# Position terms of an attention kernel: the row axis copied straight from PSUM, the column axis alone through DRAM

## The chip, the cores and the metric

The kernel runs on one NeuronCore of a Trainium2 chip. The metric is the device time of one execution in microseconds (us). Before the change it is 4188.24 us, the median of 3 runs that range from 4181.4 to 4191.72 us. The engines are TensorE (PE: matmuls; PEld: its weight loads), VectorE (DVE), ScalarE (ACT), GpSimd (POOL) and SyncE (SP), which here only issues DMAs. An engine takes its instructions in the order in which the program gave them to it. All data are float32.

## The reference

Two layers, each for 4 images of 32 x 32 tokens with 768 channels. A layer normalizes its input by groups of channels, projects it to queries, keys and values of 12 heads of 64, and attends over all 1024 tokens of an image. To the scores it adds two position terms, one for the distance in rows and one for that in columns, each a product of the query with a table of 63 relative distances (27 in layer 1, with the ends repeated):

```python
x = x + _L0_conv_ref(_gn(x), ...)          # layer 0; layer 1 is alike, with biases
# inside a layer, B*12 heads, S = H*W = 1024 tokens
rel_h = einsum('bhwc,hkc->bhwk', r_q, Rh)  # Rh[i, j] = rel_pos_h[i - j + H - 1]
rel_w = einsum('bhwc,wkc->bhwk', r_q, Rw)
bias = (rel_h[..., :, None] + rel_w[..., None, :]).reshape(B * hn, S, S)
attn = softmax(scale * einsum('bqc,bkc->bqk', q, k) + bias)
out = einsum('bqk,bkc->bqc', attn, v) ... @ Wproj + bproj
```

## The kernel before, in words

There are 8 images to work through (4 images, 2 layers), each with 6 pairs of heads; a pair is g = 0 to 47. A pair has 8 blocks of 128 queries, n = 0 to 7, and the main loop (line 705) goes through the 384 steps (g, n). The whole order is written out by hand: every engine's queue is filled in the order of this loop.

**One step (g, n).** `biases` (line 452) builds the sum of both position terms for the step after next on GpSimd, two operations of 128 x 1024. `scores` (line 466) does the matmuls of the next step; VectorE evicts them with the bias and the row's minimum (line 482), ScalarE takes the exponential and its sum (line 486). `turn` (line 501) transposes the step's attention weights in 32 x 32 blocks on VectorE into a buffer tb (line 513); after two steps, a quarter of the pair, SyncE writes tb to a DRAM scratch td (line 516) and one or two steps later reads it back as pt (`read_back`, line 524), in the layout that the weighting wants. tb has 3 buffers, and a quarter takes two. `divide` (line 491) multiplies the next step's weights by the inverse sum, one head on GpSimd, one on ScalarE. `weigh` multiplies pt with the values on TensorE (line 543): quarters 0 and 1 of a pair in step 6, quarters 2 and 3 in step 2 of the next pair.

**Fillers.** Beside this, the steps of pair g do the projections of pair g + 1 and, in four groups per pair, the output projection of this or the last image. They are generators in a list; `take(todo, n)` draws n pieces of them, by the table `shares` with one number per step. `project_in` (line 245) projects q and k in four units; for most pairs by a scheme with sums of weights (made by `sum_weights`, line 314, on ScalarE and GpSimd in steps 6 and 7 of the pair before) and sums of inputs (`sum_input`, line 333), which is a Winograd form of the 2 x 2 block product: 7 half products in place of 8. `plain(g)` pairs, the first of each image and pair 1, don't use it. `project_values` (line 361) does the values, `project_out` (line 611) the output. In an image's fifth pair VectorE normalizes the next image's input (line 226), 12 applies of 128 x 512; in its sixth pair `sum_input` makes the input's sums.

**Position terms.** `positions(g, i)` (line 398) multiplies half of the queries with the table: 64 distances of the row axis and 64 of the column axis for each query and head, in one PSUM tile of 128 x 2 x 4 x 128 (tp, line 409; tp0 and tp1 are the two tiles of a pair). ScalarE copies it to SBUF in two parts (line 419) and writes both to a DRAM scratch tdr (line 421). `diagonals(g)` (line 428) then reads from tdr, for each query, the 32 of 64 distances that belong to it: where they start depends on the query's row or column, which a DRAM address pattern can follow. That is 2 halves x 2 heads x 2 axes x 4 partition groups of 32, 32 reads of 16 KB per pair, all on SyncE's queue (line 445).

**Order around it.** What is appended to `later` in a step runs at the start of the step after next, what is appended to `early` at the start of the next one (lines 732 and 733). `positions(g + 1, 0)` runs at the start of step 2 of pair g, `positions(g + 1, 1)` at that of step 3, `diagonals(g + 1)` at that of step 4, ahead of the read of quarter 1 (`run(behind)`, line 752) in the same step; the biases of pair g + 1 begin in step 6.

**PSUM.** Two pools of two tiles, each tile two banks: `ps_s` for scores, `ps_m` for all else (projections pj and pv, position terms tp, weighting av, output o), given out in turn. A new tile waits until the last reader of the one before the last is done.

Of the kernel before, what the change touches and what calls it, by code (L numbers as in the profile page):

```python
# [45 lines left out]
P = 128  # L47
# [18 lines left out]
def attention_blocks(ctx: ExitStack, tc: tile.TileContext, a: dict, out: bass.AP):  # L66
# [13 lines left out]
    relpool = ctx.enter_context(tc.tile_pool(name="rel", bufs=3))  # L80
# [27 lines left out]
    def spare(im):  # L108

        return y_of[im][NC:] + x_of[im][:NC]  # L110
# [134 lines left out]
    def project_in(g, unit):  # L245
# [7 lines left out]
        if plain(g):  # L253
            which, i = divmod(unit, 2)
            w, x = w_of[g, which], xs[i * NC : (i + 1) * NC]
        else:
            w, x = (
                (w_of[g, 0], xs[:NC]), (w_of[g, 4], ys[NC:]),
                (w_of[g, 3], xs[NC:]), (w_of[g, 1], ys[:NC]),
            )[unit]  # L260
        t = ps_m.tile([P, 2, HALF], FP, tag="m", name=f"pj_{g}_{unit}")
        for c in range(len(x)):
            for a in range(2):
                rows = slice(a * D, (a + 1) * D)
                nc.tensor.matmul(  # L265
                    t[:, a, :], lhsT=w[rows, c, :], rhs=x[c][rows, :],
                    start=(c == 0), stop=(c == len(x) - 1),
                )
            if c < len(x) - 1:
                yield True  # L270
# [12 lines left out]
        if plain(g):  # L283
            to = k[i]
            if which == 0:
                to, t = q[i], u
            if images[im][0] == 0:
                nc.scalar.copy(to, t[0])
            else:
                nc.scalar.activation(to, t[0], AF.Identity, bias=bias[which])  # L290
            add(to, t[1], to)
        elif unit == 0:
            nc.scalar.copy(k[0], t[0])
            add(q[0], u[1], k[0].rearrange("p a m -> p m a"), bias[0])
        elif unit == 1:
            add(k[0], t[0], k[0])
            add(k[0], t[1], k[0])
        elif unit == 2:
            add(k[1], t[0], k[0])
            add(q[1], u[1], k[1].rearrange("p a m -> p m a"), bias[0])  # L300
        else:
            add(k[1], t[0], k[1], bias[1])
            add(k[0], t[0], k[0], bias[1])
            nc.vector.tensor_tensor(k[0], k[0], t[1], ALU.subtract)
        if unit in ((0, 1) if plain(g) else (0, 2)):
            (later if g else mid).append(lambda: positions(g, 1 if unit else 0))
        if g + 1 < NPAIR:
            if unit == (1 if plain(g) else 0):
                later.append(lambda: load_w(g + 1, 0))
            if unit == 3:  # L310
                early.append(lambda: load_w(g + 1, 1))
        yield True

    def sum_weights(g):

        w = w_of[g, 0], w_of[g, 1]
        w3 = w_of[g, 3] = wpool.tile([P, NC, P], FP, tag="w3", name=f"w_{g}_3")
        w4 = w_of[g, 4] = wpool.tile([P, NC // 2, P], FP, tag="w4", name=f"w_{g}_4")

        def first():  # L320
            nc.scalar.copy(w3[TOP], w[1][LOW])

        def second():
            nc.gpsimd.tensor_tensor(w3[TOP], w3[TOP], w[1][TOP], ALU.add)
            nc.gpsimd.tensor_tensor(w3[LOW], w3[TOP], w[0][TOP], ALU.subtract)
            nc.scalar.copy(w4[TOP], w3[LOW, :3])
            nc.scalar.copy(w4[LOW], w3[LOW, 3:])
            nc.gpsimd.tensor_tensor(w3[LOW], w[0][LOW], w3[LOW], ALU.subtract)
            nc.gpsimd.tensor_tensor(w[1][TOP], w[0][TOP], w[1][TOP], ALU.subtract)

        return first, second

# [65 lines left out]
    def positions(g, i):  # L398
# [3 lines left out]
        if i == 0:  # L402
            t_of[g] = dram2.tile([S, 2 * P], FP, tag="tdr", name=f"tdr_{g}")
# [9 lines left out]
        td = t_of[g]  # L413
        for k in range(2):
            if g + 1 < NPAIR:
                t = iopool.tile([P, 2, 2, P], FP, tag="res", name=f"t_{g}_{i}_{k}")
            else:
                t = spare(g // NP)[4 + 2 * i + k].rearrange("p (j h r) -> p j h r", j=2, h=2)
            nc.scalar.copy(t, ps[:, :, 2 * k : 2 * k + 2, :].rearrange("p h j r -> p j h r"))  # L419
            at = (2 * i + k) * 2 * P  # L420
            nc.scalar.dma_start(
                out=td[at : at + 2 * P, :].rearrange("(j p) r -> p j r", p=P),
                in_=t.rearrange("p j h r -> p j (h r)"),
            )
# [3 lines left out]
    def diagonals(g):  # L428
        td = t_of[g]
        rel_of[g] = []  # L430
        for half in range(2):
            rel = relpool.tile([P, 2, 2, NT // 2, HW], FP, tag="rel", name=f"rel_{g}_{half}")
            rel_of[g].append(rel)
            for h in range(2):
                for ax in range(2):
                    for y in range(4):


                        step = P * 2 * P - (4 if ax == 0 else 0)
                        at = HW * y * 2 * P + h * P + HW - 1 + 2 * HW * ax - (y if ax == 0 else 0)  # L440
                        src = bass.AP(
                            td.tensor, td.offset + at + half * (NT // 2) * step,
                            [[2 * P - ax, HW], [step, NT // 2], [1, HW]],
                        )
                        (nc.scalar if h and not g else nc.sync).dma_start(  # L445
                            out=rel[32 * y : 32 * y + 32, h, ax, :, :], in_=src
                        )
# [4 lines left out]
    def biases(g, n):  # L452
        rel, m = rel_of[g][n // 4], n % 4
        for h in range(2):
# [6 lines left out]
                rel[:, h, 0, m, :].unsqueeze(1).unsqueeze(2).to_broadcast(shape),  # L461
                rel[:, h, 1, m, :].rearrange("p (l a) -> p a l", a=4).unsqueeze(3).to_broadcast(shape),
# [184 lines left out]
    early, mid, later, behind, behind2 = [], [], [], [], []  # L647
# [32 lines left out]
    with tc.manual_schedule(engines=ENGINES):  # L680
# [11 lines left out]
        mid.pop(0)()  # L692
        take(todo, NC)
        mid.pop(0)()
        later.pop()()
# [9 lines left out]
        for at, (g, n) in enumerate(units):  # L705
            im, pair = divmod(g, NP)
            end = im + 1 == NI
            if n == 0:
                shares = [6, 6, 0, 6, 12, 6, 0, 12] if g + 1 >= NPAIR or plain(g + 1) else [9, 6, 0, 6, 6, 6, 0, 12]
# [26 lines left out]
            if n == 5 and (im, pair) >= (0, 3):  # L736
                fetch(place[((im, 0) if pair >= 3 else (im - 1, 1)) + divmod(upto, 2)])
# [24 lines left out]
            if at + 1 < len(units):  # L762
                divide(*units[at + 1])
            if pair == 4 and not end:
                for c in {2: (0, 1), 4: (2, 3), 6: (4, 5, 6), 7: range(7, NX)}.get(n, ()):
                    apply(c % NC, c // NC)
            if g + 2 < NPAIR and not plain(g + 2) and n in (6, 7):
                if n == 6:
                    sums = sum_weights(g + 2)
                sums[n - 6]()  # L770
            if pair == NP - 1 and not end:
                sum_input(im + 1, n)
            elif g == 0 or pair == 0 and n == 0:
                sum_input(im, n if g == 0 else NT)
            elif g == 1 and n == 0:
                sum_input(0, NT)
            take(todo, share)
# [66 lines left out]
```

## Time and profile before

| | |
|---|---|
| span of the profiled execution | 4203.3 us |
| PE busy | 3588.6 us (85%) |
| DVE busy | 2791.9 us (66%) |
| POOL busy | 2379.7 us (57%) |
| ACT busy | 1678.8 us (40%) |
| DMA moved | 1089.41 MB, mean 259 GB/s; of 649495 packets 262144 are under 512 B |
| reads of tdr (line 445) | 1520 on SyncE's queue and 16 on ScalarE's, 16 KB each |
| writes of tdr (line 421) | 192, 256 KB each |

Read it so: busy time is what an engine spends in its instructions, and a share of it says little where stages with different limits follow each other. What counts is who waits at the point where the work stops. Matmul busy time includes time at a halved clock; the mean of the granted clock over the span is 0.926. A pair takes about 80 us in the middle of an image and about 95 us in its last two pairs.

### The profile page before, as it was taken

The numbers are of one execution on the slowest core, as the hardware profiler recorded it, in microseconds if no ns is written. First come the engines' busy times: TensorE is split into PE (matmuls) and PEld (weight loads), VectorE is DVE, ScalarE is ACT, GpSimd is POOL, SyncE is SP. The second block draws the span as 40 slices with busy tenths as digits, with TensorE's granted clock in tenths as the row PEclk, the third lists the DMA queues.
The fourth block names the chain that finished last, engine by engine and source line by source line (L and its number), as shares of the span: only waits on it lengthen the run. The fifth ranks groups of instructions, "written<-read, shape, count | busy, mean of one in ns | idle before, by whom it ended". The sixth has DMA issues, their size and how long they took to land.

```text
span 4203.3 us, 56667 instructions
## 1 busy us (share of the span) xinstructions
PE 3588.6 (85%) x20652; PEld 1950.1 (46%) x20652; DVE 2791.9 (66%) x4092; ACT 1678.8 (40%) x2500; POOL 2379.7 (57%) x1390
## 2 busy tenths in 40 slices
PE   6779788997889978899878997799877998879989
PEld 3444445454444544445444454445544454444544
DVE  4856676666857667576676766666766666676656
ACT  3434334343334433344433444344433444334432
POOL 3656455564656645565555655566645655456653
PEclk9889999999999988999989999899988999889999
DMA  4578767887678865778668776687776777767868
GB/s 147 204 264 289 273 223 254 305 288 272 219 276 292 298 230 207 279 283 301 225 218 299 277 282 234 224 298 276 261 248 235 281 282 255 264 217 277 286 230 296
DMA packets 649495, 1089.41 MB, mean 259 GB/s; under 512 B 262144, under 2 KB 325120, under 8 KB 600064
## 3 DMA queue, kind: packets, MB, share of 16 engines
q1 hardware_dynamic: 591968, 1033.06, 69.4%
q10 hardware_dynamic: 57248, 52.73, 3.7%
q8 instruction: 163, 2.67, 0.3%
q14 instruction: 116, 0.95, 0.1%
HBM read 585.31 MB, written 500.27 MB: 258 GB/s over the span
## 4 chain that ended last, share of the span: by engine, by line
PE 41%; DMA 17%; DVE 16%; SPq 13%; issue 6%; POOL 5%; ACT 2%; ACTq 0%; DVEq 0%; POOLq 0%
PE pj L265 13%; SPq L445 12%; PE o L619 9%; DMA pt<-td 9%; PE s L473 8%; PE av L543 7%; DVE tb L513 6%; DMA td<-tb 6%; DVE sc L482 4%; POOL sc L459 3%; PE pv L378 2%; DVE x L354 2%; DVE x L226 1%; PE tp L409 1%; DVE x L357 1%
## 5 line engine op out<-in xcount | busy, mean ns | idle before, releaser
L459 POOL TENSOR_TENSOR sc<-rel 128x1024 f32<-128x1024 f32 x768 | 1547.8, 2085 | 38.5 <-DMA rel<-tdr 35.2
L497 POOL TENSOR_SCALAR sc<-sc,sm 128x1024 f32<-128x1024 f32 x384 | 455.1, 1185 | 1672.1 <-DVE sm L493 1656.1
L513 DVE STREAM_TRANSPOSE tb<-sc 128x1024 f32<-128x1024 f32 x768 | 914.1, 1223 | 666.1 <-DMA td<-tb 666.0
L486 ACT ACTIVATE sc<-sc,sm 128x1024 f32<-128x1024 f32 x768 | 880.2, 1147 | 988.0 <-DVE sm L482 959.3
L543 PE MATMUL av<-pt,v 128*64 128x256 f32 x6144 | 843.5, 424 | 389.5 <-DMA pt<-td 380.5
L482 DVE CUSTOM_DVE_ANT_0 sc<-s,sc 128x1024 f32<-128x1024 f32 x768 | 908.1, 1220 | 179.2 <-PE s L473 115.4
L265 PE MATMUL pj<-x,w 64*128 64x512 f32 x4140 | 939.1, 599 | 60.3 <-DVE x L226 26.6
L499 ACT ACTIVATE sc<-sc,sm 128x1024 f32<-128x1024 f32 x384 | 441.0, 1148 | 1111.9 <-DVE sm L493 1111.9
L543 PEld LDWEIGHTS av<-pt,v 128*64 128x64 f32 x6144 | 485.9, 153 | 776.8 <-DMA pt<-td 437.1
L473 PE MATMUL s<-k,q 64*128 64x512 f32 x3072 | 749.3, 599 | 14.5 <-DVE sm L482 12.5
L265 PEld LDWEIGHTS pj<-x,w 64*128 64x128 f32 x4140 | 416.2, 190 | 554.9 <-issue 513.7
L619 PE MATMUL o<-attn,wo 128*128 128x512 f32 x1080 | 526.2, 641 | 143.6 <-DVE res L628 62.6
L378 PE MATMUL pv<-wv,x 64*128 64x256 f32 x4608 | 515.8, 377 | 2.4 <-DVE k L241 2.4
L378 PEld LDWEIGHTS pv<-wv,x 64*128 64x128 f32 x4608 | 448.8, 187 | 94.2 <-issue 33.6
L473 PEld LDWEIGHTS s<-k,q 64*128 64x128 f32 x3072 | 288.3, 188 | 311.3 <-issue 280.2
L619 PEld LDWEIGHTS o<-attn,wo 128*128 128x128 f32 x1080 | 211.8, 203 | 450.1 <-issue 300.2
L419 ACT COPY t<-tp 128x512 f32<-128x512 f32 x188 | 110.0, 585 | 140.5 <-PE tp L409 89.7
L241 DVE TENSOR_TENSOR k<-pj,k 128x512 f32<-128x512 f32 x173 | 117.8, 690 | 66.2 <-PE pj L265 29.4
L486 ACT ACTIVATION_READ_ACCUMULATOR sc<-sc,sm 128x1 f32 x768 | 143.2, 186 | 0.0
L393 DVE TENSOR_TENSOR v<-pv,v 128x256 f32<-128x256 f32 x192 | 81.5, 425 | 79.9 <-ACT v L390 76.5
L409 PEld LDWEIGHTS tp<-tab,q 64*128 64x128 f32 x1536 | 98.3, 187 | 40.7 <-issue 37.3
L628 DVE SCALAR_TENSOR_TENSOR res<-o,bo,res 128x512 f32<-128x512 f32 x88 | 64.2, 741 | 79.0 <-PE o L619 79.0
(56 smaller groups left out, 1634.8 us busy)
## 6 DMA issues: line engine op xcount, KB each, us to landing
td<-tb SPq DMA_DIRECT2D x384, 1024.0 KB, 6.1
pt<-td SPq DMA_DIRECT2D x382, 1024.0 KB, 7.7
tdr<-t ACTq DMA_DIRECT2D x188, 256.0 KB, 5.6
w<-in_wqk SPq DMA_DIRECT2D x96, 384.0 KB, 6.5
rel<-tdr SPq DMA_DIRECT2D x1520, 16.0 KB, 1.8
x<-in_x SPq DMA_DIRECT2D x84, 256.0 KB, 6.6
part<-res SPq DMA_DIRECT2D x84, 256.0 KB, 4.3
res<-part SPq DMA_DIRECT2D x84, 256.0 KB, 8.6
```

The source lines that it names most:

```text
L265: nc.tensor.matmul(t[:, a, :], lhsT=w[rows, c, :], rhs=x[c][rows, :], start=(c == 0), stop=(c == len(x) - 1),)
L378: nc.tensor.matmul(t[:, a, k, :], lhsT=xs[i // 2 * NC + c][rows, at * P : (at + 1) * P], rhs=w[rows, c, :], start=(c == 0), stop=(c == NC ...
L445: (nc.scalar if h and not g else nc.sync).dma_start(out=rel[32 * y : 32 * y + 32, h, ax, :, :], in_=src)
L459: nc.gpsimd.tensor_tensor(sc.rearrange("p (a k) (u l) -> p a l (k u)", a=4, l=8), rel[:, h, 0, m, :].unsqueeze(1).unsqueeze(2).to_broadcas ...
L473: nc.tensor.matmul(ps[h][:, cols], lhsT=q[rows, n * P : (n + 1) * P], rhs=k[rows, cols], start=True, stop=True,)
L482: nc.vector.tensor_tensor_reduce(out=sc, in0=ps[h], in1=sc, scale=-scale, scalar=BIG, op0=ALU.add, op1=ALU.min, accum_out=st[:, 0, h : h + 1],
L486: nc.scalar.activation(sc, sc, AF.Exp, bias=st[:, 0, h : h + 1], scale=-1.0, accum_out=st[:, 1, h : h + 1],)
L497: nc.gpsimd.tensor_scalar(sc, sc, st[:, 2, h : h + 1], 1.0, ALU.mult, ALU.mult)
L499: nc.scalar.activation(sc, sc, AF.Copy, scale=st[:, 2, h : h + 1])
L513: nc.vector.transpose(tb[:, :, j, :], sc_of[g, n, h])
L543: nc.tensor.matmul(av[rows, at * 2 * P : (at + 1) * 2 * P], lhsT=v_of[g][:, k, rows], rhs=pt_of[g, quarter, h][:, :, k, :], start=(k == 0) ...
L619: nc.tensor.matmul(t, lhsT=wo_of[im, o, c], rhs=attn_of[im * NP + c, i], start=(c == c0), stop=(c == c1 - 1),)
```

## The change

It has four parts.

1. **Row axis.** The shift of the row axis depends only on the row of the token, and 32 tokens of a row lie on 32 neighbouring partitions. So ScalarE can copy each row's 32 distances straight from PSUM: 4 blocks x 4 rows, 16 copies of 32 partitions x (2 x 32) for each half, into tiles rel0. They are put in a list `last`, which runs after `divide` in the same step.
2. **Column axis.** Only the column half of the product goes through DRAM: one copy and one write per half in place of two, and 8 reads of 32 KB per pair in place of 32 of 16 KB, into tiles rel1.
3. **Sum S4.** The tile of half sums w4 is gone. Its first half is written over weights that are used up: after unit 0 of the projection ScalarE copies it into w0, and GpSimd subtracts from w0's lower half (`sum_weights_last`); its second half is read where it lies in w3. Unit 1 moves from step 0 to step 1 (`shares`), and the next w0 is loaded after unit 2.
4. **Order.** `take` comes before `sum_input` in a step; in step 7 of an image's fifth pair the five applies are interleaved with pieces of the fillers; `fetch`, which loads output weights and residuals, moves from step 5 to step 4.

It takes work from SyncE's queue and DRAM, saves SBUF, and gives ScalarE 32 small copies per pair.

```diff
-    relpool = ctx.enter_context(tc.tile_pool(name="rel", bufs=3))
+    rel0pool = ctx.enter_context(tc.tile_pool(name="rel0", bufs=3))
+    rel1pool = ctx.enter_context(tc.tile_pool(name="rel1", bufs=2))
...
-            w, x = (
-                (w_of[g, 0], xs[:NC]), (w_of[g, 4], ys[NC:]),
-                (w_of[g, 3], xs[NC:]), (w_of[g, 1], ys[:NC]),
+            w0, w1, w3 = w_of[g, 0], w_of[g, 1], w_of[g, 3]
+            w, x = (
+                ((w0, w0), xs[:NC]), ((w0, w3[:, 3:]), ys[NC:]),
+                ((w3, w0), xs[NC:]), ((w1, w1), ys[:NC]),
             )[unit]
...
+            sum_weights_last(g)
...
-            if unit == (1 if plain(g) else 0):
+            if unit == (1 if plain(g) else 2):
                 later.append(lambda: load_w(g + 1, 0))
...
-            nc.scalar.copy(w4[TOP], w3[LOW, :3])
-            nc.scalar.copy(w4[LOW], w3[LOW, 3:])
-            nc.gpsimd.tensor_tensor(w3[LOW], w[0][LOW], w3[LOW], ALU.subtract)
...
+    def sum_weights_last(g):
+        w0, w3 = w_of[g, 0], w_of[g, 3]
+        nc.scalar.copy(w0[TOP, :3], w3[LOW, :3])
+        nc.gpsimd.tensor_tensor(w0[LOW], w0[LOW], w3[LOW], ALU.subtract)
...
-        for k in range(2):
-            ...
-            nc.scalar.copy(t, ps[:, :, 2 * k : 2 * k + 2, :].rearrange("p h j r -> p j h r"))
-            nc.scalar.dma_start(...)
+        nc.scalar.copy(t, ps[:, :, :, D:].rearrange("p h j r -> p j h r"))
+        nc.scalar.dma_start(
+            out=t_of[g][i * HALF : (i + 1) * HALF, :].rearrange("(j p) r -> p j r", p=P),
+            in_=t.rearrange("p j h r -> p j (h r)"),
+        )
+
+        def rows_axis():
+            rel = rel_of[g][i] = rel0pool.tile([P, 2, 4, HW], FP, tag="rel0", name=f"rel0_{g}_{i}")
+            for j in range(4):
+                for y in range(4):
+                    of, at = slice(32 * y, 32 * y + 32), HW - 1 - 4 * (4 * i + j) - y
+                    nc.scalar.copy(rel[of, :, j, :], ps[of, :, j, at : at + HW])
+
+        last.append(rows_axis)
...
-        for half in range(2):
-            for h in range(2):
-                for ax in range(2):
-                    for y in range(4):
-                        ...
+        for h in range(2):
+            for y in range(4):
+                src = bass.AP(
+                    td.tensor, td.offset + HW * y * P + h * D + HW - 1,
+                    [[P - 1, HW], [P * P, NT], [1, HW]],
+                )
+                (nc.scalar if h and not g else nc.sync).dma_start(
+                    out=rel_of[g][2][32 * y : 32 * y + 32, h, :, :], in_=src
+                )
...
-                shares = [6, 6, 0, 6, 12, 6, 0, 12] if ... plain(g + 1) else [9, 6, 0, 6, 6, 6, 0, 12]
+                shares = [6, 6, 0, 6, 12, 6, 0, 12] if ... plain(g + 1) else [6, 9, 0, 6, 6, 6, 0, 12]
...
-            if n == 5 and (im, pair) >= (0, 3):
+            if n == 4 and (im, pair) >= (0, 3):
                 fetch(...)
...
             turn(g, n)
             if at + 1 < len(units):
                 divide(*units[at + 1])
+            run(last)
             if pair == 4 and not end:
                 for c in {2: (0, 1), 4: (2, 3), 6: (4, 5, 6), 7: range(7, NX)}.get(n, ()):
+                    if n == 7 and c % 2 == 0:
+                        take(todo, 3)
+                        share -= 3
                     apply(c % NC, c // NC)
...
+            take(todo, share)
             if pair == NP - 1 and not end:
                 sum_input(im + 1, n)
...
-            take(todo, share)
```

## The prediction

> **What bounds the kernel now.** I read the chain of waits on the page first, then the list of waits, then the timeline of one pair, then the busy time in short windows of it.
>
> The chain that ended last, by engine and by line:
>
> ```profile
> PE 41%; DMA 17%; DVE 16%; SPq 13%; issue 6%; POOL 5%; ACT 2%; ACTq 0%; DVEq 0%; POOLq 0%
> PE pj L265 13%; SPq L445 12%; PE o L619 9%; DMA pt<-td 9%; PE s L473 8%; PE av L543 7%; DVE tb L513 6%; DMA td<-tb 6%; DVE sc L482 4%; POOL sc L459 3%; PE pv L378 2%; DVE x L354 2%; DVE x L226 1%; PE tp L409 1%; DVE x L357 1%
> ```
>
> TensorE is the largest part, as it should be, but 12% of 4203 us, 504 us, is SyncE's queue issuing the reads of line 445, and 15% more is two transfers of the weights' transposition, td and pt, which stand in the same queue. The list of waits shows who suffers (waiter, releaser, us in total, times, longest):
>
> ```profile
> DVE tb L513 <- DMA td<-tb: 666.0, 49, 20.0
> PE av L543 <- DMA pt<-td: 380.5, 91, 11.0
> POOL sc L459 <- DMA rel<-tdr: 35.2, 2, 33.7
> ```
>
> GpSimd, for which line 445 reads, hardly waits: its data are early enough. VectorE waits 666 us, about once a pair, for a buffer that a late write holds, and TensorE 380 us for a late read. The timeline of one ordinary pair (start, us, engine, line), SyncE's queue and then TensorE, shows why:
>
> ```profile
> 788.83 1.49 SPq L516 DMA_DIRECT2D td<-tb  x2
> 790.41 19.19 SPq L445 DMA_DIRECT2D rel<-tdr  x32
> 809.71 0.36 SPq L129 DMA_DIRECT2D w<-in_wqk  x1
> 810.12 0.98 SPq L524 DMA_DIRECT2D pt<-td  x2
> 816.39 3.05 SPq L516 DMA_DIRECT2D td<-tb  x2
> ...
> 782.25 1.16 PE L409 MATMUL tp<-tab,q 64*128 64x128 f32 x16
> 783.24 1.89 PE L473 MATMUL s<-k,q 64*128 64x512 f32 x8
> 784.96 5.32 PE L265 MATMUL pj<-x,w 64*128 64x512 f32 x24
> 790.11 1.88 PE L473 MATMUL s<-k,q 64*128 64x512 f32 x8
> 791.83 5.35 PE L378 MATMUL pv<-wv,x 64*128 64x256 f32 x48
> ...
> 805.72 3.67 PE L543 MATMUL av<-pt,v 128*64 128x256 f32 x32
> 816.37 1.11 PE L543 MATMUL av<-pt,v 128*64 128x256 f32 x2 [6.97 <-DMA pt<-td]
> 819.10 5.64 PE L543 MATMUL av<-pt,v 128*64 128x256 f32 x30 [1.62 <-DMA pt<-td]
> ```
>
> The write of quarter 1 went out at 788.83; its read is queued behind 32 small reads and leaves only at 810.12. TensorE, dense until 809.39, then waits. The window view of 809.40 to 819.10 (us, PE busy, PEld, DVE, ACT, POOL, PE clock, DMA share, GB/s):
>
> ```profile
> 809.40:819.10 9.70, 1.12 (x3) 0.29 (x3) 0.06 (x1) 0.18 (x2) 0.00 (x0) 0.68 0.90 300
> ```
>
> All compute engines stand still, and the clock falls: the second half of the weighting takes 6.7 us where the first took 3.67. It ends at 824.74 instead of 809.39 + 3.67 = 813.06: **11.7 us lost per pair**.
>
> **What the Trainium skill says.** "Perfetto Trace Analysis", What "DMA-bound" means, names the issuing sequencer, its track solid with DMA slices, as a limit of its own: the 19.19 us above. "TensorE: Matmul & The Clock Gate", What's actually happening: the clock halves after an idle window of about 3.4 us. The trace agrees and is stricter: of the full-speed TensorE gaps of 2.5 to 3.0 us, 7 of 9 were followed by a half clock, mostly 3.4 us long; of those of 3.0 to 3.5 us, 6 of 6. "PSUM — Partial Sum Buffer", Engine vs sequencer instructions: matmuls start in program order, so one that waits for a PSUM buffer holds back all behind it; above, every other engine's work follows TensorE's.
>
> **The change, part by part.**
>
> *Reads, 32 to 8 per pair.* Line 445 issues at a median of 430 ns, and the 32 took 19.19 us with waits. Eight, each with twice the rows, take 8 x 0.43 = 3.4 to 8 x 0.86 = 6.9 us. The residual loads (wo and res, 3.3 us of issue) now stand ahead of the quarter's read, but even so: 790.4 + 6.9 + 0.4 + 3.3 = 801.0, landing by 809.5 at the 8.5 us that the later of the two reads took. It is needed at 809.4, later still with the stalls below. So the 11.7 us go, and VectorE's write leaves when its transpose is done.
>
> *Rows axis on ScalarE.* Each call of positions drops one of two 585 ns copies and one DMA issue, and adds 16 copies of 32 partitions x 64. The nearest rows:
>
> ```profile
> L419 ACT COPY t<-tp 128x512 f32<-128x512 f32 x188 | 110.0, 585 | 140.5 <-PE tp L409 89.7
> L390 ACT COPY v<-pv 128x256 f32<-128x256 f32 x100 | 36.6, 366 | 33.1 <-DVE v L393 25.5 <-PE pv L378 7.4
> 757.56 0.51 ACT L326 COPY w<-w 64x384 f32<-64x384 f32 x1 [3.72 <-POOL w L325]
> 758.09 0.51 ACT L327 COPY w<-w 64x384 f32<-64x384 f32 x1
> 1038.38 0.62 ACT L342 COPY x<-x 64x512 f32<-64x512 f32 x1
> 1038.90 0.61 ACT L351 COPY x<-x 64x512 f32<-64x512 f32 x1
> ```
>
> From 512 and 256 elements, 219 ns per 256, so 64 cost about 202 ns. Neighbours on the same partitions (342, 351) overlap by 0.1 us; where the target half changes (326, 327) they don't: 25 ns pass. The new copies change partitions each time, so I take 227 ns each, 3.65 us for 16; if they overlap, 0.1 us each, 1.7 us. Upper bound: "ScalarE: Activation LUTs", Rules for kernel authors, about 0.3 us plus 0.83 ns per element, 0.353; with the gap 0.378 and 6.05 us. No trace row here has this shape.
>
> Their total, 48 x 32 x 0.227 = 349 us, would hide on ScalarE (40% busy). What doesn't hide is the PSUM tile. The copies come after divide, and the pool of these tiles has two buffers: tp0, av, tp1, pj, pv alternate. So tp1 waits for tp0's last copy: divide ends at 781.29 (780.14 + 1.15), copies at 784.97, against 782.25: stall 2.7 us. Queued behind tp1 on TensorE are the next scores, for which VectorE, ScalarE and all else wait. Then pv waits for tp1's copies: from the end of s, 0.14 + 2.44 (two score evictions) + 2.28 (transposes) + 0.2 + 1.15 (divide) + 3.65 = 9.9 us, where TensorE has 6.9 us of work (785.13 to 791.99): stall 3.0 us. Each likely halves the clock for 3.4 us, 1.7 us lost: 0.9 (the second stall counts from s, so only tp and s are slowed) and 1.4 at these odds. Sum **8.0 us per pair**.
>
> *S4, smaller sums.* Removed: one 0.51 us copy on ScalarE per pair; one GpSimd op of 1.8 us moves to after the first projection unit. Unit 1 must now wait for a 0.51 us copy into w0 after that unit's last matmul; behind it on TensorE are units 1 and 2. It is hidden by the scores between them (1.9 us, against 0.57 + 0.51 us on ScalarE). The subtraction on GpSimd has s and unit 1, over 4 us, to finish. I cost both at 0 to 0.3 us.
>
> *Order.* In an image's fifth pair the five norm applies (6.56 us on VectorE) held a projection's eviction: TensorE stood 6.6 us (1003.25 to 1009.87). Interleaved, VectorE's own work bounds from 971.0 on: transposes 2.37, three applies 3.96, attention 0.67, scores 2.43, four evictions 3.0, transposes 2.37, applies 6.56, so the next scores at 992.4 instead of 1016.93: 24.6 us, less 8.0, is 16.6. In the sixth pair VectorE's sum_input (7.16 us for two of its operations alone) held the attention's eviction until 1092.99 while TensorE stood from 1085.14 to 1093.72, and so it went on into the next image. Without the wait for tb (1073.3 to 1082.35) VectorE goes through the same work without a break, and by the same addition the first tp group of the next image would start at 1118.3 instead of 1126.33: 8 us, which the 8.0 us of new stalls take back. Fetch one step earlier, the later weight load and the smaller pools stay at zero: SyncE is free by then.
>
> Sum: 33 ordinary pairs (four in each of 7 images, five in the last) x (11.7 - 8.0) = 122; 7 x 16.6 = 116. 4188 - 238 = **3950 us**.
>
> **The rivals.** *Copies overlap* (0.1 us each): stalls of 0.8 and 1.1 us, no half clock, 2 us per pair: 33 x 9.7 + 7 x 22.6 + 7 x 6 = 520, so 3668. For it: ScalarE's other neighbours overlap; against: none does here with a change of partitions. *Copies at the page's price*: stalls 5.2 and 5.4 us, half clocks 2.9, 13.4 per pair: 33 x 1.7 + 7 x 5.4 lost, 7 x 11.2 won, so **4204**, slower; against it, the rows above are cheaper than that price. *The read still late*: with 5 us of transfers ahead of it on the same DMA engines (share 0.90 there), 11.7 - 5 - 8 = -1.3: 33 x 1.3 + 7 x 5 lost, 7 x 11.6 won, 4185, no change.
>
> **How the numbers follow.** Main case 0.52, overlap 0.25, dear copies 0.13, late read 0.10. The range runs from 3660, the overlap case, to 4100, part of the way to the dear cases. Faster 0.87: the first two and part of the others, which lie near zero; same 0.05; slower 0.08.
>
> **What would show it.** L445 near 380 issues, and its share of the chain gone; the waits of L513 and L543 below 100 us together; 1536 small ScalarE copies at a mean near 200 ns; new TensorE waits at L409 and L378 on ScalarE, near 130 us each. If these two waits are small, the overlap case holds; if L543 still waits for pt, the late read.

## The result and the profile after

| kernel | median us | runs, us | ratio to before, 95% interval |
|---|---|---|---|
| before | 4189.98 | 4 runs, 4181.40 to 4203.27 | |
| after | 4011.60 | 4 runs, 4008.21 to 4013.65 | 0.9571 [0.9544, 0.9597] |

The change takes 178 us off, 4.3%. The forecast was 3950 us, which would have been 238 us off. The profiled execution of after spans 4011.9 us, 191 us less than the one of before (4203.3, the slowest of its four runs), and its mean granted clock is 0.941 instead of 0.926.

Where a line number of before and after differ in what follows, they belong together so: reads of tdr L445 and L452, read of a quarter (pt) L524 and L531, transposes L513 and L520, weighting L543 and L550, position terms L409 and L416, values L378 and L384, scores L473 and L480.

The chain of waits of after, by engine and by line:

```profile
PE 51%; DVE 22%; ACT 12%; issue 8%; DMA 5%; POOL 2%; DVEq 0%; SPq 0%; ACTq 0%; POOLq 0%
PE pv L384 12%; PE s L480 11%; PE pj L268 10%; DVE tb L520 9%; PE o L626 9%; ACT rel L436 7%; PE av L550 6%; DVE sc L489 6%; ACT sc L506 3%; PE tp L416 3%; DMA pt<-td 2%; DMA td<-tb 2%; DVE x L355 1%; DVE x L363 1%; DVE x L360 1%
```

SyncE's queue, 13% of the chain before, is gone, and the two transfers td and pt fall from 15% to 4%. In their place stands ScalarE with 12%, of which 7% are the new copies (L436), and the values' projection, which was 2% of the chain, is 12% of it. The list of waits (waiter, releaser, us in total, times, longest) says the same from the side of those who suffer:

```profile
PE tp L416 <- ACT rel L436: 104.9, 46, 2.7
PE pv L384 <- ACT rel L436: 98.1, 39, 2.5
DVE tb L520 <- DMA td<-tb: 28.0, 17, 5.0
PE av L550 <- DMA pt<-td: 4.5, 3, 2.0
```

VectorE's wait for tb was 666.0 us and is 28.0. TensorE's wait for pt was 380.5 us and is 4.5. What is new are two waits of TensorE for the small copies, about once a pair each, 203 us together. The group of these copies (count, us in total, mean ns of one, idle time before) has just the duration that was taken for one copy:

```profile
L436 ACT COPY rel<-tp 32x64 f32<-32x64 f32 x1536 | 310.9, 202 | 17.8 <-ACT t L424 0.9
```

The timeline of one ordinary pair (start, us, engine, line; in brackets the wait and its releaser), ScalarE, then TensorE, then SyncE's queue:

```profile
742.35 3.42 ACT L436 COPY rel<-tp 32x64 f32<-32x64 f32 x16
...
756.34 3.41 ACT L436 COPY rel<-tp 32x64 f32<-32x64 f32 x16
...
745.83 1.21 PE L416 MATMUL tp<-tab,q 64*128 64x128 f32 x16 [2.35 <-ACT rel L436]
746.82 3.58 PE L480 MATMUL s<-k,q 64*128 64x512 f32 x8
...
755.38 1.88 PE L480 MATMUL s<-k,q 64*128 64x512 f32 x8
...
759.80 7.14 PE L384 MATMUL pv<-wv,x 64*128 64x256 f32 x48 [2.54 <-ACT rel L436]
...
775.48 7.13 PE L550 MATMUL av<-pt,v 128*64 128x256 f32 x64
...
755.65 7.41 SPq L452 DMA_DIRECT2D rel<-tdr  x8
...
766.46 0.98 SPq L531 DMA_DIRECT2D pt<-td  x2
```

Three things are to be seen. The eight reads take 7.41 us of the queue, the read of pt leaves at 766.46, and the weighting from 775.48 on is one dense run of 64 matmuls in 7.13 us, where before it broke into parts with 6.97 and 1.62 us of waiting. The second tile of position terms starts at 745.83, 0.06 us after the first tile's last small copy ends (742.35 + 3.42), and the values' projection at 759.80, 0.05 us after the second tile's last copy. And both waits halve the clock behind them: the same scores take 3.58 us after the first wait and 1.88 without one, the values 7.14 us after the second wait, against 5.35 before the change. The window from 746.00 to 750.40 (us, PE busy, PEld, DVE, ACT, POOL, clock, DMA share, GB/s):

```profile
746.00:750.40 4.40, 4.40 (x26) 2.38 (x28) 0.00 (x0) 0.59 (x1) 0.42 (x1) 0.61 0.50 177
```

TensorE is busy without a break here, at a clock of 0.61. A list of busy times would not show this loss.

**By pair.** The time from VectorE's first transpose of a pair to that of the next, taken from the traces, us. The means are over images 2 to 8, those of the 5th and 6th pair over images 2 to 7, since the last image has no next one to prepare:

| pair of the image | 1st | 2nd | 3rd | 4th | 5th | 6th | first image, all six |
|---|---|---|---|---|---|---|---|
| before | 85.7 | 80.7 | 81.0 | 81.4 | 96.3 | 94.0 | 522.7 |
| after | 79.8 | 78.4 | 78.2 | 78.4 | 81.0 | 99.5 | 494.8 |
| gain | 5.9 | 2.3 | 2.8 | 3.1 | 15.3 | -5.5 | 27.9 |

The fifth pair brings about half of the gain, the ordinary pairs most of the rest, and every sixth pair gives 5.5 us back.

### The profile page after: what moved, and what is told of

The parts are those of the page before. It is cut to its first block, busy times and chain, and to the rows that moved or that the text cites. A ratio compares the mean times of both kernels' runs of the same rounds, so it can differ in the third digit from the quotient of the medians.

```text
span 4011.9 us, 56045 instructions
## 1 busy us (share of the span) xinstructions
PE 3625.1 (90%) x20652; PEld 1978.1 (49%) x20652; DVE 2783.9 (69%) x4092; ACT 1908.5 (48%) x3901; POOL 2367.4 (59%) x1390
## 4 chain that ended last, share of the span: by engine, by line
PE 51%; DVE 22%; ACT 12%; issue 8%; DMA 5%; POOL 2%; DVEq 0%; SPq 0%; ACTq 0%; POOLq 0%
PE pv L384 12%; PE s L480 11%; PE pj L268 10%; DVE tb L520 9%; PE o L626 9%; ACT rel L436 7%; PE av L550 6%; DVE sc L489 6%; ACT sc L506 3%; PE tp L416 3%; DMA pt<-td 2%; DMA td<-tb 2%; DVE x L355 1%; DVE x L363 1%; DVE x L360 1%
## 5 line engine op out<-in xcount | busy, mean ns | idle before, releaser
L466 POOL TENSOR_TENSOR sc<-rel,rel 128x1024 f32<-128x1024 f32 x768 | 1555.7, 2093 | 40.6 <-DMA rel<-tdr 34.3
L489 DVE CUSTOM_DVE_ANT_0 sc<-s,sc 128x1024 f32<-128x1024 f32 x768 | 909.4, 1221 | 370.0 <-PE s L480 346.4
L268 PE MATMUL pj<-x,w 64*128 64x512 f32 x4140 | 964.5, 612 | 75.9 <-DVE x L228 26.7
L520 DVE STREAM_TRANSPOSE tb<-sc 128x1024 f32<-128x1024 f32 x768 | 911.3, 1222 | 29.1 <-DMA td<-tb 28.0
L480 PE MATMUL s<-k,q 64*128 64x512 f32 x3072 | 837.3, 646 | 51.6 <-DVE sm L489 51.3
L550 PE MATMUL av<-pt,v 128*64 128x256 f32 x6144 | 687.5, 381 | 10.9 <-DVE q L243 6.3
L384 PE MATMUL pv<-wv,x 64*128 64x256 f32 x4608 | 581.0, 410 | 98.1 <-ACT rel L436 98.1
L384 PEld LDWEIGHTS pv<-wv,x 64*128 64x128 f32 x4608 | 486.8, 206 | 223.3 <-ACT rel L436 130.4
L550 PEld LDWEIGHTS av<-pt,v 128*64 128x64 f32 x6144 | 434.4, 137 | 293.5 <-issue 51.5
L480 PEld LDWEIGHTS s<-k,q 64*128 64x128 f32 x3072 | 314.7, 201 | 386.3 <-issue 294.1
L436 ACT COPY rel<-tp 32x64 f32<-32x64 f32 x1536 | 310.9, 202 | 17.8 <-ACT t L424 0.9
L416 PE MATMUL tp<-tab,q 64*128 64x128 f32 x1536 | 122.5, 301 | 104.9 <-ACT rel L436 104.9
L416 PEld LDWEIGHTS tp<-tab,q 64*128 64x128 f32 x1536 | 110.7, 206 | 148.1 <-ACT rel L436 125.8
```

Source lines behind the costliest of these rows:

```text
L268: nc.tensor.matmul(t[:, a, :], lhsT=w[a][rows, c, :], rhs=x[c][rows, :], start=(c == 0), stop=(c == len(x) - 1),)
L384: nc.tensor.matmul(t[:, a, k, :], lhsT=xs[i // 2 * NC + c][rows, at * P : (at + 1) * P], rhs=w[rows, c, :], start=(c == 0), stop=(c == NC ...
L436: nc.scalar.copy(rel[of, :, j, :], ps[of, :, j, at : at + HW])
L466: nc.gpsimd.tensor_tensor(sc.rearrange("p (a k) (u l) -> p a l (k u)", a=4, l=8), rel0[:, h, :].unsqueeze(1).unsqueeze(2).to_broadcast(shape),
L480: nc.tensor.matmul(ps[h][:, cols], lhsT=q[rows, n * P : (n + 1) * P], rhs=k[rows, cols], start=True, stop=True,)
L489: nc.vector.tensor_tensor_reduce(out=sc, in0=ps[h], in1=sc, scale=-scale, scalar=BIG, op0=ALU.add, op1=ALU.min, accum_out=st[:, 0, h : h + 1],
```

## The experiments

The theory tested first: what stands in the way of the rest of the gain is neither ScalarE's time nor the DMAs, but the PSUM tile that the small copies hold until after divide. Four edits of the copies tell this apart; then come the reads, the order, S4, and the versions that put together what was found. Ratios are to the kernel before, which was run again with each group of experiments: its medians were 4196 to 4197 us there and 4189.98 with after, so a difference of a few us between kernels of different groups means nothing.

**Copies early.** The small copies run at once, behind the copy of the column half.

```diff
-        last.append(rows_axis)
+        rows_axis()
```

> The changed kernel with one line moved: the 16 row-axis copies of a half run right after the column half's copy and its write, not after divide. ScalarE does the same work. Theory 1 (the PSUM tile is held too long, because the copies stand behind divide): the waits of tp and pv on the copies (104.9 and 98.1 us on TensorE) all but vanish, with the half clocks after them; 8.4 us per ordinary pair come back, less about 1 us because the read of pt is then needed earlier: about 3670 us (3630 to 3720). The exponentials start up to 1.4 us later in two steps of eight, which costs under 0.5 us each. Theory 2 (ScalarE's added time itself costs, wherever it stands): no gain, about 4010 us.

Measured: 3782.5 us, ratio 0.9018 [0.8998, 0.9037]. The same copies on the same engine, only earlier, take another 229 us off, more than the 178 us of the whole change. An ordinary pair takes 72.6 to 73.4 us instead of 78.2 to 78.4. Both waits for L436 leave the head of the list. But the time is 112 us above what the theory gave, and the list of waits says where it is:

```profile
PE av L550 <- DMA pt<-td: 90.8, 51, 3.4
```

With TensorE faster, the read of pt comes too late again, by at most 3.4 us at a time, and VectorE's wait for tb grows from 28.0 us to 172.9. The held tile was the cause of its stalls; the size was overstated, since the next limit lay closer than I had it.

**Copies from SBUF.** The whole tile is copied to SBUF at once, by one more copy of 128x512 per half, and the small copies, still after divide, read from there.

```diff
+        r = iopool.tile([P, 2, 4, D], FP, tag="res", name=f"r_{g}_{i}")   # last pair: a spare tile
...
+        nc.scalar.copy(r, ps[:, :, :, :D])
...
-                    nc.scalar.copy(rel[of, :, j, :], ps[of, :, j, at : at + HW])
+                    nc.scalar.copy(rel[of, :, j, :], r[of, :, j, at : at + HW])
```

> The changed kernel, but both halves of tp are copied to SBUF at once, two copies of 585 ns as in the kernel before, and the 16 row-axis copies read that SBUF copy, still after divide. ScalarE has 96 copies of 585 ns more (56 us) and slower small copies (SBUF as source, about 240 ns). Theory 1 (held PSUM tile): the waits of tp and pv vanish as in the run with the copies moved: about 3680 us. Theory 2 (ScalarE's time): slower than the changed kernel, 4030 to 4100 us.

Measured: 3789.39 us, ratio 0.9029 [0.8994, 0.9063]. By the groups of ScalarE's copies it works longer, and the kernel is as fast as with the copies early:

```profile
L441 ACT COPY rel<-r 32x64 f32<-32x64 f32 x1504 | 363.8, 242 | 16.5
L429 ACT COPY r<-tp 128x512 f32<-128x512 f32 x94 | 55.7, 592 | 0.0
```

A small copy takes 242 ns in place of 202, and the 128x512 copies are an addition. So ScalarE's time is not what cost after; the hold of the tile is.

**Groups outermost.** The two loops of the copies change places, so that four copies in a row stay on the same 32 partitions. Everything else is as in after, the place after divide too.

```diff
-            for j in range(4):
-                for y in range(4):
+            for y in range(4):
+                for j in range(4):
```

> The changed kernel with the two loops around the small copies exchanged: four copies in a row on the same 32 partitions, so that the partitions change 4 times in 16 and not 16 times. Theory (a copy on other partitions than the one before it can't overlap with it): 12 of 16 copies start about 0.1 us after the one before, the 16 take about 2.2 us and not 3.4, both stalls shrink to about 1.2 us, below what brings a half clock: about 5.5 us less per pair, 3760 us. Rival (short copies don't overlap in any order): 16 copies in 3.4 us, 4011 us.

Measured: 3823.91 us, ratio 0.9112 [0.9085, 0.9138]. The order of two loops alone is worth 188 us. One half's copies in the timeline of an ordinary pair, and TensorE around them:

```profile
714.72 2.13 ACT L436 COPY rel<-tp 32x64 f32<-32x64 f32 x16
...
716.90 1.16 PE L416 MATMUL tp<-tab,q 64*128 64x128 f32 x16 [1.06 <-ACT rel L436]
717.89 1.89 PE L480 MATMUL s<-k,q 64*128 64x512 f32 x8
...
727.89 5.45 PE L384 MATMUL pv<-wv,x 64*128 64x256 f32 x48 [1.25 <-ACT rel L436]
```

One copy still takes 201 ns, but 16 of them take 2.13 us, not 16 x 0.201 = 3.2. In the trace they start 92 to 113 ns apart where the partitions stay the same and 208 to 218 ns where they change; in after, where they change each time, 213 to 217 ns (197 behind the first). So the hold shrinks by 1.3 us, and the two waits of the pair from 2.35 and 2.54 us to 1.06 and 1.25; in the list of waits of the whole run they fall by 109 us together (203.0 to 94.1). More comes off in the matmuls behind them: the scores take 1.89 us here and took 3.58 in after, the values 5.45 and took 7.14. A wait of 1.06 or 1.25 us left the clock alone, one of 2.35 or 2.54 us did not; none of the 88 full-speed gaps of 1.00 to 1.25 us in this trace was followed by a half clock within 3 us. Waits and half clocks come to 6.0 us a pair, and the 2nd to 4th pairs fall by 4.9 to 5.2. The run ends 64 us above the 3760 expected; TensorE's wait for pt is back, 32.5 us in the list, but what else stands there was not taken apart.

**Four copies per half.** One copy per group of 32 partitions takes all four blocks by an address pattern whose step from block to block is 124 instead of 128 elements. The place after divide stays.

```diff
-            for j in range(4):
-                for y in range(4):
-                    of, at = slice(32 * y, 32 * y + 32), HW - 1 - 4 * (4 * i + j) - y
-                    nc.scalar.copy(rel[of, :, j, :], ps[of, :, j, at : at + HW])
+            for y in range(4):
+                of, at = slice(32 * y, 32 * y + 32), HW - 1 - 16 * i - y
+                one = ps[of, 0, 0, at : at + HW]
+                part = one.ap[0]
+                src = bass.AP(one.tensor, one.offset, [part, [4 * P, 2], [P - 4, 4], [1, HW]])
+                nc.scalar.copy(rel[of], src)
```

> The changed kernel with 4 copies of 32 partitions x (2 x 4 x 32) in place of 16 of 32 x (2 x 32): the start of the window moves by 4 from block to block, so one address pattern with a stride of 124 does four blocks. Theory 1 (length of the hold): 4 copies of about 366 ns, 1.5 us in place of 3.4; stalls of about 0.5 us, no half clock, 7 us less per pair: about 3690 us. Rival (the wait is set by something else than the copies' length, as the place behind divide alone): 4000 us.

Measured: 3785.57 us, ratio 0.9023 [0.9003, 0.9043].

```profile
L437 ACT COPY rel<-tp 32x256 f32<-32x256 f32 x384 | 137.7, 358 | 4.3 <-ACT t L424 0.9
```

Four copies take 1.47 us per half, and that is short enough: the tile is free almost when TensorE wants it. As with the copies early, the gain over after is 226 us, where 322 was expected, and the ordinary pair stops at the same 72.7 us. Three edits that share nothing but an earlier end of the hold (early, from SBUF, four copies) end within 7 us of each other.

**32 reads again.** Each of the 8 reads is cut into 4 of a quarter of the rows; nothing else changes against after.

```diff
+                for k in range(4):
                     src = bass.AP(
-                        td.tensor, td.offset + HW * y * P + h * D + HW - 1,
-                        [[P - 1, HW], [P * P, NT], [1, HW]],
+                        td.tensor, td.offset + HW * y * P + h * D + HW - 1 + 2 * k * P * P,
+                        [[P - 1, HW], [P * P, 2], [1, HW]],
                     )
...
```

> The changed kernel with its 8 column-axis reads cut into 32 of a quarter of the rows each: the same bytes and descriptors, four times the issues. Theory 1 (the gain comes from SyncE's issue time): the reads take about 19 us on the queue as before and not 7.4; the read of pt leaves 11 us later and lands 7 us after it is needed, with a half clock: 9 us more per pair, 4430 us (4330 to 4450), and VectorE waits for tb again. Theory 2 (the gain comes from half the bytes and packets): 4011 us.

Measured: 4434.09 us, ratio 1.0564 [1.0536, 1.0592]; 4430 was expected. From the list of waits, and from the timeline of a pair:

```profile
PE av L551 <- DMA pt<-td: 355.0, 94, 10.2
...
829.24 16.32 SPq L453 DMA_DIRECT2D rel<-tdr  x30
```

The same bytes, moved by more instructions, bring the wait for pt back, 355 us, and the waits for the small copies stay as they were (104.3 us for tp, 104.9 in after). So the change is a trade of two things: fewer reads bring 422 us (4434 to 4012), and the rest of it, by difference, stalls against gains in order, takes 244 us back (4190 to 4434).

**Sum of inputs before the fillers.** `sum_input` goes back ahead of `take`, as in before.

```diff
-            take(todo, share)
             if pair == NP - 1 and not end:
                 sum_input(im + 1, n)
...
+            take(todo, share)
```

> The changed kernel with one part undone: sum_input comes before take again, as in the kernel before. Theory 1 (with take first, VectorE idles for the evictions of matmuls that are still running and does the input's sums only afterwards, ahead of the next scores): an image's sixth pair, 99.5 us in the changed kernel and 94.0 before, gets back to 90 to 94 us, the others stay: about 3965 us. Theory 2 (the sixth pair lost its 5.5 us to the stalls of the row-axis copies, as every pair): 4011 us, sixth pair still above 98 us.

Measured: 3929.24 us, ratio 0.9363 [0.9349, 0.9378]. The sixth pair falls from 99.5 to 91.6 us, below before's 94.0, and the first pair of the next image from 79.8 to 77.1. The timeline of VectorE, GpSimd and TensorE in a sixth pair of after, and then VectorE in the experiment, shows two effects:

```profile
1014.79 0.42 DVE L399 TENSOR_TENSOR v<-pv,v 128x256 f32<-128x256 f32 x1 [1.47 <-ACT v L396]
...
1016.11 2.37 DVE L355 TENSOR_TENSOR x<-x,x 64x512 f32<-64x512 f32 x1
...
1015.97 4.43 POOL L466 TENSOR_TENSOR sc<-rel,rel 128x1024 f32<-128x1024 f32 x2
...
1022.18 4.92 PE L480 MATMUL s<-k,q 64*128 64x512 f32 x8 [1.55 <-DVE sm L489]
```

```profile
1006.40 0.68 DVE L355 TENSOR_TENSOR x<-x,x 64x512 f32<-64x512 f32 x1
```

In after VectorE first evicts what `take` put into the queue, idling for it (1.47 us here), and only then does the sums, with the scores' eviction (L489) queued behind them; TensorE, which needs the scores' PSUM tile, stands. And the sum that takes 0.68 us in the experiment takes 2.37 us here, because it starts 0.14 us after GpSimd has begun the biases (L466) of the next step. The Trainium skill, "SBUF — State Buffer", SBUF: two separate sides, says of VectorE operations with two SBUF inputs and GpSimd operations that whichever starts first holds their shared ports to its end. The trace agrees: here L355 ends 0.44 us after the first of the two GpSimd operations. In all of after it took 0.66 to 0.69 us in the 17 cases where no GpSimd operation was under way at its start; in the 31 others it ended, at the median, 0.45 us after that operation. By the groups of VectorE, L355 has a mean of 1557 ns in after and 672 ns in the experiment; the three sums together cost VectorE 219.3 us there and 175.6 us here, 5.5 us for each of 8 images. In before the three cost 219.8 us. So the longer sums are a part of why this order beats both, but not of why after is worse than before in this pair. The place in the queue is what remains for that; it is argued from the timeline and was not run by itself.

**Applies interleaved, in before.** The part of the change that concerns the fifth pair alone, put into the kernel before.

```diff
+                    if n == 7 and c % 2 == 0:
+                        take(todo, 3)
+                        share -= 3
                     apply(c % NC, c // NC)
```

> The kernel before with one part of the change alone: in step 7 of an image's fifth pair the five applies are interleaved with pieces of take. Theory 1 (the applies hold the projection's eviction, 6.6 us of TensorE's time and a half clock): the fifth pair, 94 to 97 us, loses 7 to 9 us: 4130 us, and about as much of the changed kernel's 15.3 us in that pair is due to it. Theory 2 (the fifth pair gained from SyncE's queue alone): 4190 us.

Measured: 4147.04 us, ratio 0.9884 [0.9866, 0.9902]. The fifth pair falls from 96.3 to 89.2 us, and no other kind by more than 0.5. That is about 7 of the 15.3 us that the fifth pair gains in after; the other 8 come with the reads and the rest.

**S4 alone, in before.** The first half of the half sums over w0, unit 1 in step 1, the next w0 loaded after unit 2. The swapped order of the two lists in `spare`, which belongs to this part, is left out: in an image's fifth pair unit 1 then reads tiles into which the next image is being loaded, and that pair's time is not to be read.

```diff
-            nc.scalar.copy(w4[TOP], w3[LOW, :3])
-            nc.scalar.copy(w4[LOW], w3[LOW, 3:])
-            nc.gpsimd.tensor_tensor(w3[LOW], w[0][LOW], w3[LOW], ALU.subtract)
...
+    def sum_weights_last(g):
+        w0, w3 = w_of[g, 0], w_of[g, 3]
+        nc.scalar.copy(w0[TOP, :3], w3[LOW, :3])
+        nc.gpsimd.tensor_tensor(w0[LOW], w0[LOW], w3[LOW], ALU.subtract)
...
```

> The kernel before with the part S4 alone (no tile w4, the half sum written over w0 after unit 0, unit 1 in step 1, the later weight load). Theory (the copy into w0 is hidden by the scores, 0 to 0.3 us per pair are lost, one ScalarE copy less): 4190 to 4205 us, no change beyond 0.3%. Rival (unit 1 waits for the copy, 0.5 us and more in each of 39 pairs): 4210 us and above.

Measured: 4223.78 us, ratio 1.0076 [1.0058, 1.0093]. The 2nd to 4th pairs take 81.7 to 81.9 us, 0.5 to 1.0 more than before (of the 1st pairs, 4.1 us shorter behind a fifth pair 4.3 us longer, nothing is read), and the wait that I had costed at next to nothing is there, at the first use of the new half in unit 1:

```profile
PEld pj L266 <- ACT w L334: 34.7, 32, 3.4
PE pj L266 <- ACT w L334: 9.2, 30, 2.5
```

The rival stated ahead was right in the cost: S4 costs 0.5 to 1.0 us in a pair that uses it. The wait for the copy is a part of that: the weight loads (PEld) wait 34.7 us, but in part while matmuls still run, and the matmuls themselves 9.2 us, 0.3 us a time. What the rest is (unit 1's new place, the later load) was not taken apart.

**All three together.** Copies early, four per half, sums before the fillers.

> The changed kernel with the copies moved ahead, four copies in place of 16, and sum_input before take. If the parts add up: about 3670 less 7 to 9 us for each of 7 sixth pairs, about 3610 us (3570 to 3680); pt's wait is then the next bound, so less than the sum of the single gains. If one of them only hides another, no better than the best of them alone.

Measured: 3691.54 us, ratio 0.8796 [0.8782, 0.8811]: 320 us below after, where 330 to 440 was expected. The ordinary pair takes 72.5 to 73.1 us, no less than with one remedy of the copies alone, and the wait for pt is back, 90.3 us in the list:

```profile
711.28 1.09 SPq L532 DMA_DIRECT2D pt<-td  x2
...
722.99 5.35 PE L551 MATMUL av<-pt,v 128*64 128x256 f32 x30 [2.22 <-DMA pt<-td]
```

The 8 reads end at 707.88. Between them and the read of pt lie 3.4 us, of which 2.8 are the loads of output weights and residuals (`fetch`) that the change moved from step 5 into this step 4. Hence three orders of the queue.

**The loads back in step 5**, with all three:

```diff
-            if n == 4 and (im, pair) >= (0, 3):
+            if n == 5 and (im, pair) >= (0, 3):
                 fetch(...)
```

> The kernel with the three edits together (3691 us), with fetch back in step 5 as in the kernel before. There the read of pt is late again: TensorE waits 3.2 us per ordinary pair (719.8 to 723.0), and the half clock costs 2.4 more. Theory 1 (the residual loads ahead of it on the queue make it late, 2.7 us of issue and 1.4 MB on the same DMA engines): the read leaves 2.7 us earlier, the wait falls below 1 us, about 4 to 5 us per pair: about 3490 us. Theory 2 (the reads of line 453, 7.1 us for 8, make it late on their own, or the loads only move in front of the next write): above 3640 us.

Measured: **3594.93 us**, ratio 0.8574 [0.8557, 0.8591], the best of this study: 14.3% less than before, 10.4% less than after.

```profile
700.62 7.13 PE L551 MATMUL av<-pt,v 128*64 128x256 f32 x64
```

The weighting is dense again (the wait for pt is down to 2.7 us in the list), the ordinary pair takes 69.8 to 70.3 us, TensorE is busy 95% of the span at a mean clock of 0.984. The 97 us gained are fewer than the 200 expected: the pt wait was worth 2.8 us a pair and not 4 to 5.

**The read of pt first**, ahead of the 8 reads and the loads in step 4, with all three:

```diff
+            if n == 4:
+                run(behind)
...
-            run(behind)
+            if n != 4:
+                run(behind)
```

> The kernel with the three edits together, with the read of pt in step 4 issued ahead of the position reads, the weight load and fetch. It then leaves as soon as the quarter's write has landed, about 5.5 us earlier, and the position data come about 6 us later. Theory 1 (only the place in SyncE's queue makes it late): no wait for pt at all, about 3480 us. Theory 2 (GpSimd needs the position data at that time): the wait moves to the biases, no better than 3640 us.

Measured: 3663.06 us, ratio 0.8737 [0.8719, 0.8755], a miss: 28 us gained of the 210 expected. TensorE's wait for pt is down to 1.6 us, but another takes its place:

```profile
DVE tb L521 <- DMA td<-tb: 237.8, 45, 9.4
```

It was 174.5 us with the order of "all three" and 159.5 with the loads in step 5. VectorE now waits longer for a later write of tb, and the output projection then waits for VectorE (103.5 us for attn, 32.6 with "all three"). SyncE's queue in step 4 of a pair shows what the read does there:

```profile
691.75 1.46 SPq L524 DMA_DIRECT2D td<-tb  x2
697.31 2.81 SPq L532 DMA_DIRECT2D pt<-td  x2
700.22 5.67 SPq L453 DMA_DIRECT2D rel<-tdr  x8
```

The read stands right behind the write that it reads back, so the queue does nothing from 693.21 to 697.31, until the first of the quarter's two writes has landed (at 697.25), waits again for the second (699.70), and only then issues the eight reads and the loads. At the median over the pairs the queue has issued all that stands between the writes of quarters 1 and 2 after 17.6 us, against 11.9 with "all three" and 12.8 with the loads in step 5. The next write, the first of quarter 2, lands 11.1 us after that quarter's last transpose on average, against 9.6 and 9.1, and in all three kernels it is this write for which VectorE waits: the transpose starts 0.09 us after it has landed, at the median.

**Both orders**, the read first and the loads in step 5:

> Both of the last two edits. If the read's place is all, fetch no longer matters: the same as the run with the read first, about 3480 us within 15. If the loads also delay the position reads or the next write of tb, some 10 to 30 us better than that run.

Measured: 3665.78 us, ratio 0.8739 [0.8721, 0.8757], the same as the read first alone. So it is not the loads that make the read-first order slow; with both, quarter 2's write lands 11.0 us after the last transpose. That the time goes into VectorE's wait for tb, and that the waiting read delays what is behind it in the queue, is read from the traces; an order in which the read goes ahead without waiting was not run.

## Why the prediction was right, and what in it was off

The side was right, the time within the range, 62 us (1.5%) below what was measured. By its steps:

- **The bound of before** was right. The 32 reads in SyncE's queue are what held the read of pt: given back to after they cost 422 us, forecast to 4 us.
- **Reads, 32 to 8.** L452 has 380 issues as predicted; its part of the chain is gone, and the waits for tb and pt are down to 28.0 and 4.5 us. The 8 reads took 7.41 us in the pair shown, more than the 3.4 to 6.9 stated (6.2 at the median over the pairs), and no harm came of it in after, because TensorE was late as well. In the faster versions it does matter.
- **The copies.** 1536 of them at 202 ns, as predicted, 3.42 us for 16 against 3.65. The upper price worked out from the Trainium skill, "ScalarE: Activation LUTs", Rules for kernel authors, 0.353 us for one, was too high: that row prices an ACTIVATE whose bias is a pointer operand, and these copies took 0.202. That neighbours overlap only on the same partitions was read from two pairs of rows; the exchange of two loops showed it.
- **The held tile.** Waits of 104.9 and 98.1 us in place of near 130 each; per pair 2.35 and 2.54 us in place of 2.7 and 3.0. The half clocks were undersized: I gave them the odds of 7 in 9, and they came within 3 us after 79 of the 85 full-speed gaps of 2.25 to 2.75 us that I counted in after's trace. They cost 3.58 - 1.88 = 1.7 and 7.14 - 5.35 = 1.8 us, not 0.9 and 1.4. "TensorE: Matmul & The Clock Gate", What's actually happening, has an idle window of about 3.4 us; here the measurement decides, and these shorter gaps were mostly enough. Sum 2.35 + 1.7 + 2.54 + 1.8 = 8.4 against 8.0: two errors that nearly cancel.
- **S4** was costed at 0 to 0.3 us and costs 0.5 to 1.0. I had held ScalarE's copy against the scores that lie between the units, but TensorE still waits for it (in after the matmuls wait 19.9 us in 38 pairs, 0.5 us each). With the 8.4 this fits what the 2nd to 4th pairs gain, 2.3 to 3.1 us and not 3.7: 11.7 - 8.4 - 0.5 to 1.0 is 2.3 to 2.8.
- **Fifth pair:** 15.3 against 16.6. The sum put all of it under the order of the applies; alone they give about 7, and the rest came with the reads.
- **Sixth pair: the step that failed.** "8 us, which the 8.0 us of new stalls take back" is 0; measured is -5.5. I took it that VectorE would go through its work without a break once the wait for tb was gone. But with `take` ahead of `sum_input` VectorE has breaks: it idles for the fillers, and the sums then stand ahead of the scores' eviction. Turned round, the sixth pair gains 7.9 us. Up to 5.5 us of this are sums that no longer wait for GpSimd; how the 5.5 us lost against before divide between place and other delays was not taken apart further. Six such pairs at 5.5 are 33 of the 62 us. The ordinary pairs (28 at about 0.2), the fifth pairs (6 at 1.3) and the first image (27.9 in place of 4 x 3.7 + 16.6 = 31.4) give another 17; the rest is within what the two profiled runs and the medians differ by.

The rivals: had the copies overlapped, 3668 was forecast. The two loops exchanged, which halves the steps between most copies, gave 3824, with the sixth pair's loss still in it, so that rival was too hopeful about how soon the next limit comes. Of the other two, the dear copies are refuted by the 202 ns and the late read by the 4.5 us of waiting for pt.

## What to carry to other kernels

When work is moved off a queue, ask what buffer the new reader holds, and from when: here the copies' own time cost little (from the SBUF copy it was longer and the kernel faster), but reading a shared PSUM tile after other work on the same engine cost 8 us a pair, and one line's place was worth more than the whole change. Look for the half clock behind a TensorE wait in the duration of the same matmuls, since busy time does not show it: here a wait of 2.35 us cost 4.05 with it, one of 1.06 us only itself. And when instructions that wait for another engine are put ahead of instructions that don't, on an engine that works in order, the second kind inherits the wait.

## What the runs showed of the hardware that I had not expected

- ScalarE's short copies of 32 x 64 from PSUM start 92 to 113 ns apart on the same partitions and 208 to 218 ns apart where the partitions change (medians by position), at the same 201 ns each: 16 take 2.13 us in one order of two loops and 3.41 us in the other.
- One copy of 32 x 256 took 358 ns, four of 32 x 64 on the same partitions about 0.53 us (16 in 2.13 us), in changing order 0.85 us (16 in 3.41 us). From SBUF the copy of 32 x 64 took longer than from PSUM, 242 ns against 202.
- TensorE gaps of 2.25 to 2.75 us at full clock were followed by a half clock within 3 us in 79 of 85 cases (after), gaps of 1.00 to 1.25 us in none of 88 (groups outermost).
- A VectorE sum of two SBUF tiles that takes 0.66 to 0.69 us alone ended 0.45 us (median) after the GpSimd operation that was under way when it started, in 31 cases.
